# The inner layer of the second block's MLP in two groups of four products on four row tiles

## The chip, the cores and the metric

The kernel runs on one core of a Trainium2 chip. The metric is the device time of one launch in microseconds (us). TensorE (PE in the profile) multiplies into PSUM; VectorE (DVE) and ScalarE (ACT) read PSUM and work in SBUF; GpSimd (POOL) works in SBUF; SyncE (SP) issues DMAs. Each engine runs its own instructions in order, and engines wait for each other by semaphores.

## The reference

The input x has 32 sequences of 128 tokens of 144 numbers. Three transformer blocks follow each other, with a rotation between the first and the second. Each block is adaptive layer norm, attention with 16 heads of 9 numbers, and an MLP of width 576. The third block has a mixture of four experts as its MLP. What matters here is the second block (`L2`):

```python
ada = silu(c) @ W_ada + b_ada
shift_msa, scale_msa, gate_msa, shift_mlp, scale_mlp, gate_mlp = split(ada, 6)
h = modulate(layernorm(x), shift_msa, scale_msa)
x = x + gate_msa * attention(h, W_qkv, b_qkv, W_proj, b_proj)
h = modulate(layernorm(x), shift_mlp, scale_mlp)
mlp = gelu(h @ W_fc1 + b_fc1, approximate=True) @ W_fc2 + b_fc2
x = x + gate_mlp * mlp
```

## The kernel before

**Tiling.** All is float32. A sequence (128 tokens) is one step of attention; four sequences are a group (`G = 4`), so every block has eight groups (`NG = 8`). The MLP's inner layer and the projection to q and k are done for a whole group: a product gives 128 output channels for 4 x 128 tokens, one PSUM bank of 128 x 512. The width 576, a row for the bias of the outer layer and padding make five such chunks (`NFC = 5`); the fifth is half full.

**Main and rest.** The 144 input channels are more than TensorE's 128 rows. So each product is a main one over 128 channels (`hM`) and a rest over the other 16 and the bias (`hR`), accumulated in one bank. A rest needs 32 rows only. `hR` and the rest weights lie in four copies of 32 rows each, and a rest names one of the four row tiles (`rows4(k)`), so that rests on different tiles can run together. `both` (L716) issues a list of main products and a list of rests, rests first or main products first. Chunk m of the MLP uses tile `m % 3`; the three products of q and k use tiles 0, 1 and 2.

**PSUM.** One bank is for the weighted values (`ps_o`); seven banks are handed out in turn by `bank` (L82) to everything else. A tile waits for the last reader of the bank that it is given.

**The order.** It is written out by hand. The loop at L1439 runs over ticks; a tick has one sequence in each of three stages of attention. In order it issues the first half of `scores` (the maxima's products `ps_s` of one sequence and the exponentials' products `ps_w` of the one before; DVE takes the negated maxima `nm`, L930, and ACT the exponentials, L934), `weigh` (L940), the second half of `scores`, then `largest_T` (L867: PE transposes `nm`) and `largest` (L872: DVE adds it to q). Between these are named gaps, in order: a, e, t, first half of scores, stats, weigh, o, b0, b, den, pre1, second half of scores, c, y1, y2, y3, `largest_T`, z, d. In the second and third blocks the projection of attention follows d, but in every fourth tick of the second block it comes ahead of `largest_T`. `put` (L1308) hangs a function on a tick and a gap; `put2` (L1311) hangs its two halves. `sums_by_blocks` (L970) divides by the softmax's sums on DVE: it reads `on`, which ACT copies from `ps_o` (L955), and stands ahead of the second half's `nm` in DVE's queue.

**The lines that the change touches.** t0 is the tick at which a group's attention starts. In the second block (L1387 to L1391) `mlp1`, by `fc1` (L1020), does chunks 0 to 2 in gap c of tick t0 + 8 and chunks 3 and 4 in gap c of t0 + 9, rests first in both. `fc1` then activates a dummy number (L1034), which draws the load of the Gelu table on ACT, and the chunks (L1037) into `hid`; the next exponential draws the load of the Exp table. `mlp2` (L1049, L1039) is five products per sequence, in order of m, the last with `hid[:, SHARED]`, the fifth chunk. The four sequences' `mlp2` stand at t0 + 10 in gaps b and d, and t0 + 11 in b and c. The group three later has its q and k (`qk_chunks`, L753) in gap c of t0 + 10; ACT copies them (L766 to L776), and SP's four DMAs (L779) move a part of k. In the groups with a later group to rotate, `rotate_T` (L1054), `rotate_in` (L1071) and `rotate` (L1087) stand at t0 + 8 in d and t0 + 9 in b and d. `mlp` (L1594) lays the rest weights out on the host.

Of the kernel before, what the change touches and what calls it, by code (L numbers as in the profile page):

```python
# [17 lines left out]
B, T, C = 32, 128, 144  # L18
# [6 lines left out]

SHARED = 8
NPC = 9
MLP_COLS = NFC * (128 + 128 + C)
PAIR_COLS = NPC * (256 + C)
D = 64  # L30
E = 4
G = 4
# [37 lines left out]
def tile_kernel(ctx: ExitStack, tc: tile.TileContext, a: dict, out: bass.AP):  # L70
# [675 lines left out]
    def qk_tiles(g):  # L746
# [3 lines left out]
            gr[g]["kT"] = take_kT()  # L750
        return gr[g]["qT"], gr[g]["kT"]

    def qk_chunks(g):  # L753


        p = PARAMS[g[0]]
        hM, hR = gr[g]["hM_a"], gr[g]["hR_a"]
        qT, kT = qk_tiles(g)
        pss = [bank([128, G * T], f"ps_qk_{g[0]}_{g[1]}_{m}") for m in range(3)]
        cols = [slice(128 * m, 128 * m + 128) for m in range(3)]  # L760
        yield from both(
            [(ps, p.wqk[:, c], hM) for ps, c in zip(pss, cols)],
            [(ps, p.wqkR[rows4(m), cols[m]], hR[rows4(m)]) for m, ps in enumerate(pss)],
            False,
        )
        nc.scalar.copy(qT[:, 0, :], pss[0])  # L766
        if g[0] == 1 and g[1] < 2:
            nc.gpsimd.tensor_copy(kT[:, 3, :], kmask[:, 3:4].to_broadcast([128, G * T]))
        if g == (1, 0):
            for r in (1, 2):  # L770
                nc.scalar.mul(kT[:, r, :], pss[1], kmask[:, r : r + 1])
            gr[g]["k"] = kT, pss[1]
        else:
            nc.scalar.mul(kT[:, 2, :], pss[1], kmask[:, 2:3])
            nc.scalar.copy(kT[:, 1, :], pss[1])  # L775
        nc.scalar.copy(qT[:, 1, :], pss[2])  # L776
        for j in range(4):
            r = 32 * j + 1
            nc.sync.dma_start(  # L779
                kT[r : r + HD, 3, :], qT[r + PITCH : r + PITCH + HD, 1, :]  # L780
            )
# [235 lines left out]
        layer, b, g, i = of(s)  # L1017
        residual(b, st[s].pop("pj"), gr[g]["ga"][:, i, :], f"a_{s}", layer == 0)

    def fc1(g, p, name, m, to, rest_first):  # L1020


        hM, hR = gr[g]["hM_m"], gr[g]["hR_m"]
        pss = [bank([128, G, T], f"ps_h_{name}_{m + i}") for i in range(len(to))]
        cols = [slice(128 * (m + i), 128 * (m + i) + 128) for i in range(len(to))]
        tiles = [rows4((m + i) % 3) for i in range(len(to))]
        yield from both(
            [(ps, p.w1[:, c], hM) for ps, c in zip(pss, cols)],
            [(ps, p.w1R[r, c], hR[r]) for ps, c, r in zip(pss, cols, tiles)],
            rest_first,  # L1030
        )

        t = small.tile([128, 1], F32, tag="gelu", name=f"gelu_{name}_{m}", bufs=1)
        nc.scalar.activation(t, half, AF.Gelu_apprx_tanh)  # L1034
        for ps, i in zip(pss, to):
            n = 64 if g[0] < 2 and i == SHARED else 128
            nc.scalar.activation(hid[:n, i], ps[:n], AF.Gelu_apprx_tanh)  # L1037
# [6 lines left out]
        return ps  # L1044

    def mlp1(g, m, to, rest_first):
        return fc1(g, MLPS[g[0]], f"{g[0]}_{g[1]}", m, to, rest_first)

    def mlp2(g, i):  # L1049
        b = g[1] * G + i  # L1050
# [113 lines left out]
                nc.gpsimd.tensor_tensor(acc, acc, t, ALU.add)  # L1164

    def moe1(g, pair, part, rest_first):
        to = ((0, 1, 2), (SHARED, 3, 4), (5, 6, 7))[part]
        return fc1(g, PAIRS[pair], f"3_{g[1]}_{pair}", 3 * part, to, rest_first)

    def shared_by_gate(g, pair):  # L1170

# [154 lines left out]
    for layer in range(3):  # L1326
        ahead = 5 if layer == 0 else 6
        for n in range(NG):
            g = (layer, n)
            t0 = first[layer] + n * G  # L1330
            for i in range(G):
                s = layer * B + n * G + i
                at_a = t0 + i - ahead
                if layer == 1 and n == 0:
                    at_a = t0 - 4 + i // 2
                if layer == 1 and i == 0:
                    put(at_a - 2, "d", rotate_T, n)
                    put(at_a - 1, "b", rotate_in, n)
                    put(at_a - 1, "d", rotate, n)
                stats[at_a].append((s, "a"))  # L1340
                stats[t0 + i + 3].insert(0, (s, "m"))
                if layer < 2:
                    end = at_a != t0 + i - ahead or (layer, i) == (1, G - 1)
                    put(*((at_a, "d") if end else (at_a + 1, "b")), ln_T, s, "a")
                else:
                    put(at_a, "d", ln_T, s, "a")
                if layer == 0:
                    put(t0 + i + 4, "a", ln_T, s, "m")
                else:
                    put(t0 + i + 3, "d", ln_T, s, "m")  # L1350
                if layer == 0:
                    put(t0 + i - 3, "c", qk0_project, s)
                    put(t0 + i - 3, "z", qk0_variance, s)
                    put(t0 + i - 2, "e", qk0_guess, s)
                    if s == 0:
                        for gap in "bbc":
                            put(-2, gap, qk0_newton, s, nc.vector)
                    else:
                        for gap in ("b", "c", "y2"):
                            put(t0 + i - 2, gap, qk0_newton, s)  # L1360
                    put(t0 + i - 1, "b", qk0_divide, s)
                    put(t0 + i - 1, "c", qk0_T, s)
            if layer == 0:
                for i in (0, 2):
                    put2(t0 + i // 2, "stats", "b", values, g, i, 2, True)
            elif layer == 1:
                put2(t0, "stats", "b", values, g, 0, 2, True)
                put2(t0 + 1, "stats", "b", values, g, 2, 2, True)
            else:
                put2(t0, "y2", "y2", values, g, 0, 2, True)  # L1370
                put2(t0 + 1, "den", "pre1", values, g, 2, 2)
            if layer:
                put2(t0 - 2, "c", "c", qk_chunks, g)
                if g == (1, 0):
                    put(t0 - 2, "y2", qk_masked, g)
                if g != (1, 0):
                    for r in (0, 1):
                        put(*((t0 - 2, "z") if layer == 2 and n > 2 else (t0 - 1, "a")), qk_mask, g, nc.gpsimd, r)
            if layer == 0:
                joined = t0 + 10 >= first[1]  # L1380
                put2(t0 + 10, *("cc" if joined else ("stats", "b")), mlp1, g, 0, (0, 1, 2), True)
                joined = t0 + 11 >= first[1]
                put2(t0 + 11, *("cc" if joined else "dd"), mlp1, g, 3, (3, SHARED), joined)
                for i in range(G):
                    at_ = t0 + 12 + i // 2 + ((n, i) == (NG - 1, G - 1))
                    put(at_, "bd"[i % 2] if at_ < first[1] or (n, i) == (NG - 2, G - 1) else "bc"[i % 2], mlp2, g, i)
            elif layer == 1:  # L1387
                put2(t0 + 8, "c", "c", mlp1, g, 0, (0, 1, 2), True)
                put2(t0 + 9, "c", "c", mlp1, g, 3, (3, SHARED), True)
                for i in range(G):  # L1390
                    put(t0 + (10, 10, 11, 11)[i], "bdbc"[i], mlp2, g, i)  # L1391
            else:
                put2(t0 + 7, "o", "c", gate_logits, g)
                put(t0 + 8, "e", expert_ranks, g)
                put(t0 + 8, "stats", expert_weights, g)
                for i in range(G):
                    put(t0 + 8 + i // 2, "cdab"[i], moe_bias, g, i, n == NG - 1)
                for pair in range(2):
                    at_ = t0 + 8 + 2 * pair
                    put2(at_, "stats", "b0", moe1, g, pair, 0, True)  # L1400
                    if n == NG - 1:
                        put2(at_, "stats", "pre1", moe1, g, pair, 1, True)
                    else:
                        put2(at_, "den", "pre1", moe1, g, pair, 1, False)
                    put2(at_ + 1, "stats", "b0", moe1, g, pair, 2, True)
                    put2(at_, "stats", "y1", shared_by_gate, g, pair)
                    put2(at_, "y2", "y3", moe2_parts, g, 2 * pair, 0)
                    put(at_ + 1, "b", moe2, g, 2 * pair, 1)
                    put(at_ + 1, "c", moe2, g, 2 * pair, 2)
                    put(at_ + 1, "y2", moe2, g, 2 * pair, 3)  # L1410
                    for i in range(G):
                        put(at_ + 2, "aabb"[i], moe2, g, 2 * pair + 1, i)
                        if pair and n == NG - 1:
                            put(at_ + 2, "aabb"[i], moe_out, g, i, nc.vector if i == G - 1 else nc.gpsimd)
                if n < NG - 1:
                    put(t0 + 12, "b", moe_out, g)
# [256 lines left out]
```

## Time and profile before

| what | us |
|---|---|
| median of 3 runs (lowest, highest) | 1279.36 (1277.12, 1282.75) |
| the profiled execution | 1276.88 |
| its span, first to last instruction | 1275.2 |
| a period of four ticks, second block, groups with rotation | 37.4 |
| ScalarE's table loads, all: 57 at L934 and 58 at L1034 | 73.1 and 74.4 |
| ScalarE's idle time before L1037, put down to the products of fc1 | 99.4 |
| VectorE's busy time at L930, the maxima | 246.5 |
| mean granted TensorE clock | 0.989 of full |

Busy time is summed over instructions and their overlap is taken out per engine. A line of the timeline gives start, length, engine, line, operation, output<-input, partitions x elements, count, and in brackets the idle time before it with what ended it. A float32 matmul shows as two instructions, so x6 is three products. Matmuls overlap their neighbours in the pipeline: the distance from one start to the next says more than the length.

### The profile page before, as it was taken

To read this page: it belongs to the slowest core of one execution; us is meant where nothing else is said; L and a number is where in the kernel's file an instruction comes from. 1 tells how busy PE (TensorE), PEld (TensorE's weight loads), DVE (VectorE), ACT (ScalarE), POOL (GpSimd) and SP (SyncE) were. 2 spreads that over 40 slices of the span, in tenths; PEclk is the share of its full clock that TensorE was granted. 3 is DMA by queue.
4 is the path that set the end of the run, shared out by engine and by line. 5 is a ranking of instruction groups with operands and counts; after the bars stand their busy time and mean duration, and the time that the engine had idled before them with its cause. 6 is when DMAs were issued, how large, how long until landed. Compare 5 with 4: busy or idle time off the path is not lost.

```text
span 1275.2 us, 35382 instructions
## 1 busy us (share of the span) xinstructions
PE 1226.3 (96%) x13980; PEld 898.6 (70%) x13980; DVE 808.1 (63%) x2540; ACT 779.4 (61%) x1724; POOL 667.9 (52%) x1641
## 2 busy tenths in 40 slices
PE   6889888999989999999999999999999999999998
PEld 4668666778766677767677777767676767677666
DVE  5598888877875466666666766645454646454343
ACT  2467777688776665667666666565656555555431
POOL 5567777766754444444545554626262636261610
PEclk9699999999999999999999999999999999999999
DMA  8301011010013111111121111210101010100000
GB/s 227 75 4 38 3 37 37 2 38 21 20 36 132 56 39 55 35 49 45 41 87 56 56 47 46 85 47 15 51 11 55 11 55 11 55 20 17 20 27 10
DMA packets 50328, 56.49 MB, mean 44 GB/s; under 512 B 4560, under 2 KB 35792, under 8 KB 49904
## 3 DMA queue, kind: packets, MB, share of 16 engines
q1 hardware_dynamic: 49504, 53.75, 14.2%
q8 instruction: 113, 1.85, 0.6%
q10 hardware_dynamic: 656, 0.44, 0.2%
q14 instruction: 55, 0.45, 0.1%
HBM read 39.99 MB, written 13.00 MB: 42 GB/s over the span
## 4 chain that ended last, share of the span: by engine, by line
PE 70%; DVE 4%; ACT 0%; issue 0%; POOL 0%; DVEq 0%
PE ps_h L721 20%; PE ps_f L1191 10%; PE ps_s L918 7%; PE ps_w L918 6%; PE ps_o L949 6%; PE ps_qk L721 5%; PE ps_f L1043 4%; PE ps_pj L1013 3%; PE ps_v L721 3%; PE ps_f L1196 1%; DVE nm L930 1%; PE ps_o L870 1%; PE ps_hT_m L690 1%; PE ps_cw L1179 1%; PE ps_hT_a L690 1%; PE ps_d L1092 0%
## 5 line engine op out<-in xcount | busy, mean ns | idle before, releaser
L930 DVE TENSOR_REDUCE nm<-ps_s 128x4 f32<-128x512 f32 x384 | 246.5, 683 | 95.9 <-PE ps_w L918 74.8
L934 ACT ACTIVATE pr<-ps_w 128x512 f32<-128x512 f32 x384 | 208.5, 595 | 149.7 <-PE ps_w L918 141.0
L918 PE MATMUL ps_s<-kT,qT 32*128 32x256 f32 (+2 forms) x1536 | 235.1, 409 | 0.9 <-ACT kT L850 0.9
L918 PE MATMUL ps_w<-q,kT 32*128 32x128 f32 x3072 | 230.0, 284 | 0.0
L918 PEld LDWEIGHTS ps_w<-q,kT 32*128 32x128 f32 x3072 | 194.4, 187 | 11.0 <-issue 6.2
L1037 ACT ACTIVATE hid<-ps_h 128x512 f32<-128x512 f32 (+1 forms) x224 | 120.4, 590 | 99.8 <-PE ps_h L721 99.4
L918 PEld LDWEIGHTS ps_s<-kT,qT 32*128 32x128 f32 x1536 | 136.9, 187 | 29.4 <-issue 9.2
L721 PE MATMUL ps_h<-hM_m,mlps 128*128 128x512 f32 x304 | 144.1, 607 | 0.0
L1200 DVE SCALAR_TENSOR_TENSOR acc<-ps_f,cw,acc 128x144 f32<-128x144 f32 x128 | 46.7, 365 | 146.3 <-PE ps_f L1191 71.5
L999 POOL TENSOR_TENSOR x_sb<-x_sb,res_a 128x144 f32<-128x144 f32 x96 | 46.9, 489 | 156.5 <-DVE res_a L1002 155.8
L949 PE MATMUL ps_o<-pr,vaug 128*32 128x128 f32 x3072 | 104.4, 277 | 0.0
L949 PEld LDWEIGHTS ps_o<-pr,vaug 128*32 128x32 f32 x3072 | 78.6, 110 | 32.7 <-PE ps_w L918 17.4
L721 PEld LDWEIGHTS ps_h<-hM_m,mlps 128*128 128x128 f32 x304 | 53.4, 190 | 66.9 <-issue 65.6
L1043 PE MATMUL ps_f<-mlps,hid 128*128 128x144 f32 x640 | 93.7, 294 | 0.0
L1043 PEld LDWEIGHTS ps_f<-mlps,hid 128*128 128x128 f32 x640 | 82.4, 191 | 8.8 <-issue 4.7
L934 ACT ACT_TABLE_LOAD x57 | 73.1, 1283 | 10.0 <-PE ps_w L918 9.1
L793 POOL TENSOR_SCALAR kT<-kT,cst 128x512 f32<-128x512 f32 x30 | 46.9, 1562 | 58.5 <-ACT kT L775 57.0
L1034 ACT ACT_TABLE_LOAD x58 | 74.4, 1283 | 1.0
L661 POOL TENSOR_SCALAR rs_m_a<-mv_m_a 128x2 f32<-128x2 f32 x81 | 15.5, 191 | 113.5 <-DVE mv_m_a L659 86.6
L1191 PEld LDWEIGHTS ps_f<-pair,hid 128*128 128x128 f32 x512 | 66.9, 190 | 8.4 <-issue 7.6
L701 ACT ACTIVATE hM_m<-ps_hT_m,modM 128x128 f32<-128x128 f32 x96 | 44.6, 465 | 45.8 <-PE ps_hT_m L690 43.8
L1191 PEld LDWEIGHTS ps_f<-mlps,hid 128*128 128x128 f32 x512 | 66.7, 190 | 7.9 <-issue 6.9
(336 smaller groups left out, 2756.2 us busy)
## 6 DMA issues: line engine op xcount, KB each, us to landing
gates<-gates SPq DMA_DIRECT2D x48, 288.0 KB
hD_m<-hG_m SPq DMA_DIRECT2D x24, 256.0 KB
hR_m<-hD_m SPq DMA_DIRECT2D x24, 256.0 KB
hD_a<-hG_a SPq DMA_DIRECT2D x16, 256.0 KB
hR_a<-hD_a SPq DMA_DIRECT2D x16, 256.0 KB
x_sb<-in_x SPq DMA_DIRECT2D x8, 288.0 KB
out_x<-x_sb SPq DMA_DIRECT2D x7, 288.0 KB
mlps<-in_L_mlp SPq DMA_DIRECT2D x2, 1000.0 KB
```

Source lines behind the costliest of these rows:

```text
L721: nc.tensor.matmul(ps, x, y, start=k == 0, stop=k == 1)
L793: eng.tensor_scalar(o, k, m, None, ALU.mult)
L918: nc.tensor.matmul(o, x, y, start=True, stop=True)
L930: nc.vector.tensor_reduce(to, view, AX.X, ALU.max, negate=True)
L934: nc.scalar.activation(pr[:, 4 * e : 4 * e + 4, :].rearrange("p s q -> p (s q)"), view, AF.Exp, scale=SCALE,)
L949: nc.tensor.matmul(po[rows4(j), t, :], v[:, 4 * j + 2 * t + r, :], prs[j // 2][:, 4 * (j % 2) + 2 * r + t, :], start=r == 0, stop=r == 1,)
L999: nc.gpsimd.tensor_tensor(x_sb[:, b, :], x_sb[:, b, :], t, ALU.add)
L1034: nc.scalar.activation(t, half, AF.Gelu_apprx_tanh)
L1037: nc.scalar.activation(hid[:n, i], ps[:n], AF.Gelu_apprx_tanh)
L1043: nc.tensor.matmul(ps, hid[:, at0, i, :], w2[:, m, :], start=m == 0, stop=m == NFC - 1)
L1191: nc.tensor.matmul(ps[:, 0, :], hid[:, at0 + m, i, :], w2[:, at0 + m, :], start=m == 0, stop=m == 3)
L1200: nc.vector.scalar_tensor_tensor(acc, ps[:, 0, :], w, acc, ALU.mult, ALU.add)
```

## The change

Chunks 0 to 3 of the second block's inner layer are issued together in gap c of t0 + 8, main products first, with their rests on row tiles 0 to 3. The fifth chunk is issued with q and k: `qk_chunks` of the group three later (for the last three groups, one of the first three groups of the third block) takes one more main product and one more rest, on tile 3, and after its own copies activates that chunk. Gap c of t0 + 9 is left without products. The four `mlp2` move to t0 + 10 in gap d, and t0 + 11 in b, c and d. A table `MLP_TILES` gives the row tiles; the first block's and those of the third block's first pair of experts are as before, and those of the second pair are others. The parts of `moe1` beyond 2 are not called, and the branch for the third block's MLP in `qk_chunks` isn't reached.

```diff
+MLP_TILES = {
+    "L0": (0, 1, 2, 0, 1), "L2": (0, 1, 2, 3, 3),
+    "L3_0": (0, 1, 2, 0, 1, 2, 0, 1, 2), "L3_1": (1, 2, 3, 3, 0, 1, 0, 2, 3),
+}
...
+    JOIN = {(1, n): (1, n - 3) for n in range(3, NG)}
+    JOIN.update({(2, n): (1, n + NG - 3) for n in range(3)})
...
     def qk_chunks(g):
...
-        yield from both(
-            [(ps, p.wqk[:, c], hM) for ps, c in zip(pss, cols)],
-            [(ps, p.wqkR[rows4(m), cols[m]], hR[rows4(m)]) for m, ps in enumerate(pss)],
-            False,
-        )
+        main = [(ps, p.wqk[:, c], hM) for ps, c in zip(pss, cols)]
+        rest = [(ps, p.wqkR[rows4(m), cols[m]], hR[rows4(m)]) for m, ps in enumerate(pss)]
+        f = JOIN.get(g)
+        if f is not None:
+            l, mlp, m = ("L2", MLPS[1], 4) if f[0] == 1 else ("L3_1", PAIRS[1], 3)
+            psh, main_h, rest_h = fc1_products(f, l, mlp, f"{f[0]}_{f[1]}_s", (m,))
+            main, rest = main + main_h, rest + rest_h
+        yield from both(main, rest, False)
...
         nc.scalar.copy(qT[:, 1, :], pss[2])
+        if f is not None:
+            gelus(f, f"{f[0]}_{f[1]}_s", psh, m, (SHARED,))
...
-    def fc1(g, p, name, m, to, rest_first):
+    def fc1_products(g, l, p, name, ms):
         hM, hR = gr[g]["hM_m"], gr[g]["hR_m"]
-        tiles = [rows4((m + i) % 3) for i in range(len(to))]
+        pss = [bank([128, G, T], f"ps_h_{name}_{m}") for m in ms]
+        cols = [slice(128 * m, 128 * m + 128) for m in ms]
+        tiles = [rows4(MLP_TILES[l][m]) for m in ms]
+        main = [(ps, p.w1[:, c], hM) for ps, c in zip(pss, cols)]
+        rest = [(ps, p.w1R[r, c], hR[r]) for ps, c, r in zip(pss, cols, tiles)]
+        return pss, main, rest
+
+    def fc1(g, l, p, name, ms, to, rest_first):
+        pss, main, rest = fc1_products(g, l, p, name, ms)
+        yield from both(main, rest, rest_first)
+        gelus(g, name, pss, ms[0], to)
+
+    def gelus(g, name, pss, m, to):
         t = small.tile([128, 1], F32, tag="gelu", name=f"gelu_{name}_{m}", bufs=1)
         nc.scalar.activation(t, half, AF.Gelu_apprx_tanh)
         for ps, i in zip(pss, to):
...
             elif layer == 1:
-                put2(t0 + 8, "c", "c", mlp1, g, 0, (0, 1, 2), True)
-                put2(t0 + 9, "c", "c", mlp1, g, 3, (3, SHARED), True)
+                put2(t0 + 8, "c", "c", mlp1, g, 0, (0, 1, 2, 3), False)
                 for i in range(G):
-                    put(t0 + (10, 10, 11, 11)[i], "bdbc"[i], mlp2, g, i)
+                    put(t0 + (10, 11, 11, 11)[i], "dbcd"[i], mlp2, g, i)
...
-    def mlp(name, w1, b1, w2):
+    def mlp(name, w1, b1, w2, tiles):
...
-            k, cols = m % 3, slice(128 * m, 128 * m + 128)
+            k, cols = tiles[m], slice(128 * m, 128 * m + 128)
```

More of the change, by code (lines that the diff above doesn't have):

```diff
@@ L1018, in project_sum @@
         residual(b, st[s].pop("pj"), gr[g]["ga"][:, i, :], f"a_{s}", layer == 0)
-    def fc1(g, p, name, m, to, rest_first):
+    def fc1_products(g, l, p, name, ms):
         hM, hR = gr[g]["hM_m"], gr[g]["hR_m"]
-        pss = [bank([128, G, T], f"ps_h_{name}_{m + i}") for i in range(len(to))]
-        cols = [slice(128 * (m + i), 128 * (m + i) + 128) for i in range(len(to))]
-        tiles = [rows4((m + i) % 3) for i in range(len(to))]
[L1027 to L1031, printed above, removed]
+        pss = [bank([128, G, T], f"ps_h_{name}_{m}") for m in ms]
[9 more added lines that the diff above has]
+    def gelus(g, name, pss, m, to):
         t = small.tile([128, 1], F32, tag="gelu", name=f"gelu_{name}_{m}", bufs=1)
@@ L1046, in mlp1 @@
     def mlp1(g, m, to, rest_first):
-        return fc1(g, MLPS[g[0]], f"{g[0]}_{g[1]}", m, to, rest_first)
+        ms = range(m, m + len(to))
+        return fc1(g, ("L0", "L2")[g[0]], MLPS[g[0]], f"{g[0]}_{g[1]}", ms, to, rest_first)
     def mlp2(g, i):
@@ L1166, in moe1 @@
     def moe1(g, pair, part, rest_first):
-        to = ((0, 1, 2), (SHARED, 3, 4), (5, 6, 7))[part]
-        return fc1(g, PAIRS[pair], f"3_{g[1]}_{pair}", 3 * part, to, rest_first)
+        ms = range(3 * part, 3 * part + 3)
+        if part > 2:
+            ms = ((0, 1, 2, 4), (5, 6, 7, 8))[part - 3]
+        to = [(0, 1, 2, SHARED, 3, 4, 5, 6, 7)[m] for m in ms]
+        return fc1(g, f"L3_{pair}", PAIRS[pair], f"3_{g[1]}_{pair}", ms, to, rest_first)
     def shared_by_gate(g, pair):
@@ L1609 @@
         w2 = np.vstack([w2, b2, pad[:63, :1].repeat(C, 1)])
-        mlp(l, np.hstack([w1, pad[:C]]), np.hstack([b1, pad[C]]), w2)
+        mlp(l, np.hstack([w1, pad[:C]]), np.hstack([b1, pad[C]]), w2, MLP_TILES[l])
     for n in range(2):
@@ L1619 @@
         w2 = np.vstack([w2[0][:512], w2[1][:512], w2[0][512:], w2[1][512:]])
-        mlp(f"L3_{n}", w1, b1, w2)
+        mlp(f"L3_{n}", w1, b1, w2, MLP_TILES[f"L3_{n}"])
     arrays["L3_b2"] = inputs["L3_cond_b2"].ravel()
```

## The prediction

> **What bounds the kernel now.** I read the page first: busy shares and the chain that ended last.
>
> ```profile
> PE 1226.3 (96%) x13980; PEld 898.6 (70%) x13980; DVE 808.1 (63%) x2540; ACT 779.4 (61%) x1724; POOL 667.9 (52%) x1641
> ...
> PE 70%; DVE 4%; ACT 0%; issue 0%; POOL 0%; DVEq 0%
> ```
>
> TensorE (PE) sets the time: anything PE waits for is paid in full, and removed PE work is gained only if nothing else ends later. So I walked one 4-tick period of the second block in the timeline, engine by engine. It repeats every 37.4 us (tables of windows: 37.26 of 37.40 us PE busy in three of them). I name ticks by their distance from t0 of the MLP's own group: T8 to T11. PE first (start us, length us, engine, line, op, out<-in, shape, count):
>
> ```profile
> 511.51 1.07 PE L721 MATMUL ps_h<-hR_m,mlps 32*128 32x512 f32 x6
> 512.50 2.84 PE L721 MATMUL ps_h<-hM_m,mlps 128*128 128x512 f32 x6
> 515.18 0.27 PE L870 MATMUL ps_o<-cst,nm 128*128 128x128 f32 x1
> ...
> 521.72 1.02 PE L721 MATMUL ps_h<-hR_m,mlps 32*128 32x512 f32 x4
> 522.67 1.98 PE L721 MATMUL ps_h<-hM_m,mlps 128*128 128x512 f32 x4
> 524.50 0.27 PE L870 MATMUL ps_o<-cst,nm 128*128 128x128 f32 x1
> ...
> 528.76 1.49 PE L1043 MATMUL ps_f<-mlps,hid 128*128 128x144 f32 x10
> ...
> 534.06 1.14 PE L721 MATMUL ps_qk<-hR_a,L_wqkR 32*128 32x512 f32 x6
> 535.13 0.33 PE L870 MATMUL ps_o<-cst,nm 128*128 128x128 f32 x1
> 535.29 1.39 PE L1043 MATMUL ps_f<-mlps,hid 128*128 128x144 f32 x10
> 536.52 0.27 PE L690 MATMUL ps_hT_m<-cst,xh_m 128*128 128x128 f32 x1
> ```
>
> From start to next start: rests of three chunks 0.99, of two 0.95, of q and k 1.07; a main product about 0.9; one mlp2 1.23 to 1.42. L870 is the transpose of the row maxima nm, after which PE does the rest of its tick. In T9 the two fc1 chunks (521.72 to 524.50) stand just before it, and cover this on VectorE (DVE):
>
> ```profile
> 520.50 0.45 DVE L974 STREAM_TRANSPOSE block<-on 128x256 f32<-128x256 f32 x1
> ...
> 522.17 1.28 DVE L930 TENSOR_REDUCE nm<-ps_s 128x4 f32<-128x512 f32 x2
> ```
>
> nm is ready at 523.45, 1.7 us after the scores end. Last ScalarE (ACT):
>
> ```profile
> 512.89 1.28 ACT L1034 ACT_TABLE_LOAD   x1
> 514.18 0.20 ACT L1034 ACTIVATE gelu<-half 128x1 f32<-128x1 f32 x1
> 514.29 1.69 ACT L1037 ACTIVATE hid<-ps_h 128x512 f32<-128x512 f32 x3
> ...
> 517.83 1.28 ACT L934 ACT_TABLE_LOAD   x1 [0.86 <-PE ps_w L918]
> ...
> 535.22 0.58 ACT L766 COPY qT<-ps_qk 128x512 f32<-128x512 f32 x1 [2.64 <-PE ps_qk L721]
> ```
>
> The load back to Exp waits for PE's scores; it isn't hidden. The four copies of q and k take 2.0 us (535.22 to the next op at 537.22).
>
> **The change, step by step** (group at 511.51; each figure is how much later, +, PE then stands than before).
>
> PE work alone: three groups of rests, 0.99 + 0.95 + 1.07 = 3.01, become two of four. No row shows four tiles of 512 columns; between 0.95 (two tiles) and 1.07 + 0.9 = 1.97 (the fourth alone), nearest the rows of three: I take 1.1 each. Saved: 0.8 us a group, 6.5 us in eight. All main products, mlp2s, gelus (five a group) and table loads (two each way) remain, so the rest is order.
>
> *T8 and T9.* With the rests last, all four chunks end together, at 511.51 + 3.6 + 1.1 = 516.2; before, the first gelu ran at 514.29, during the main products. Now four gelus, 0.53 apart, end at 518.4; then come hM_m and, in the groups with a rotation, xM and xR, queued behind them on ACT, which took 1.10 us, to 519.5. Only then the Exp load (1.28), the two Exps (1.09) and the copy of on, which starts 0.1 before they end and takes 0.38: 522.1. DVE's block to nm takes 2.95 (520.50 to 523.45): nm is there at 525.1, against PE's transpose at 524.50 before. That is +0.65, though PE has 1.9 us less to do by then: T9's fc1 chunks, its cover, are gone. Four h tiles hold four of seven PSUM banks; if the next scores wait for the last gelu and for hM_m, PE is 1.3 later at the scores, the chain about 0.7 later: +1.35. I take +1.0. In the four groups without rotation (h at 661.27, transpose at 673.25 before) the same sum gives +1.05.
>
> [...]
>
> *T10.* The first mlp2 leaves gap b: -1.42. A wait of 0.35 in its scores (526.40 to the weighing at 527.75, against 1.0 normally) goes, since no gelu stands before them on ACT: -0.35 in rotated groups. The q and k group has a fourth main product, +0.92, and +0.03 of rests. PE is at the transpose at +0.2.
>
> *The stall I count most on.* In gap d, right behind the transpose, stands the first mlp2. Its fifth product reads hid[SHARED], which now comes from this same group of products. ACT needs for it 0.09 + 2.0 (four copies) + 1.28 (Gelu load) + 0.11 + 0.59 = 4.07 us from the end of the products; PE has 0.16 (transpose) + 0.98 (four products). It waits 2.9 us, with the transposes of hT_m, the projection and the next scores queued behind it: +3.1 at T11.
>
> *T11.* ACT's load back to Exp again waits for ps_w, so the Exps are 1.28 later than PE is, then on, block, nm: nm ready at about 547.4, PE there at 547.45. A tie; before, PE waited 0.1 there. Then the mlp2 moved from T10's b to here, +1.42, less 0.45, since it covers the wait of the next scores for q (544.62 to 546.17, 1.55 instead of 1.1).
>
> Sum of a group: 1.0 - 1.42 - 0.35 + 0.95 + 2.95 + 0 + 1.42 - 0.45 = +4.1; without rotation 0.4 more, +4.5. 4 x 4.1 + 4 x 4.5 = +34 us. The saving of 0.8 is in it already.
>
> At no cost: the DMAs of kT stay behind qT's last copy on SP, POOL's masks of kT behind ACT's copies, which keep their place; hG_m with its two DMAs comes about 4 us later, and hR_m is wanted two ticks (18 us) on; without that cover PE would wait the same 4. mlp2's residuals come a gap later, and the third block's statistics read x_sb more than ten ticks on. The third block's other row tiles (24 groups of rests) may overlap the scores' tail more or less, 0.1 us each by the overlaps around 508.30: between -2.4 and +2.4, taken as 0.
>
> *Clock.* Idle PE is slowed here. At 78.95 to 80.73 it waited for DVE, and (window, its us, PE, PEld, DVE, ACT, POOL busy, then PEclk):
>
> ```profile
> 79.00:80.00 1.00, 0.00 (x0) 0.00 (x0) 0.86 (x6) 0.69 (x2) 0.90 (x3) 1.00 0.00 0
> ...
> 83.00:84.00 1.00, 1.00 (x17) 0.78 (x11) 0.93 (x4) 0.00 (x0) 0.94 (x3) 0.50 0.00 0
> 84.00:85.00 1.00, 1.00 (x11) 0.90 (x8) 0.96 (x5) 0.84 (x2) 0.81 (x3) 0.94 0.00 0
> ```
>
> 1.77 us of idling were followed by 3.1 us at half clock (80.85 to 83.95), at most 1.55 us lost; a wait of 1.38 at 58.5 had none. Waits of 2.9 and 1.8 us a group can each set it off: 0 to 3.1 us. ACT's lag in T11 hides part; I take 0.5, +4 in all.
>
> [...]
>
> **The sum.** The profiled execution took 1276.88 (span 1275.2 and 1.7 around it), 2.5 under the median of 1279.36. 1276.9 + 34 + 4 = 1315.
>
> **Rivals.** *The saving arrives* (faster): PE loses 0.8 a group, the waits are covered: 1276.9 - 6.5 = 1270. For it: 96% PE, a chain of PE alone. Against: the fifth product's wait is a data dependence on an in-order queue. It needs ACT's 4.07 us to shrink to 1.9: no row does.
> *Half clock after both waits*, in all groups: 1277 + 34 + 25 = 1336. For it: the 1.77 us row; against: ACT's lag covers part.
> *Tiles don't run together*, what the change says not done: 2 x 0.9 more a group, +14: 1329. Against: two tiles 0.95, three 0.99.
> *Small loss*: the T8/T9 wait vanishes and only 2.5 of the last remain: 4.1 - 1.0 - 0.45 = 2.65 a group, 1298.
> *Break-even*: the waits just eat the 0.8: 1277.
>
> **How the numbers follow.** Forecast 1302 to 1326: 0.65. Half clock or serial tiles: 0.14. Small loss (from 1284): 0.11. Break-even 0.03. Faster 0.07. A measurement tells about 0.5%, 6.4 us, from no change: slower 0.90, same 0.03, faster 0.07. The range reaches from under the small loss to within the rivals above: 1295 to 1333.
>
> **What would show it.** PE's L870 in T9 waiting 1 to 2.5 us for nm; the last product of the first mlp2 waiting about 3 us for hid after a Gelu load that stands behind the copies of q and k; period 41 to 42 us instead of 37.4; PE busy share down to about 93%. Wrong if hid[SHARED] is there within 2 us of the q and k products, if nm is ready in T9 when the scores end, or if the rests of four take over 1.5 us.

## The result, and the profile after

| | us |
|---|---|
| median after, 6 runs (lowest, highest) | 1336.41 (1333.23, 1345.06) |
| median before, beside it, 6 runs (lowest, highest) | 1281.03 (1277.12, 1284.04) |
| ratio, 95% interval | 1.0448 (1.0412 to 1.0485) |
| the profiled execution after, its span | 1345.06, 1343.4 |

The changed kernel is slower by 55 us. That is the direction of the forecast, but above its range, which ended at 1333. The profiled execution happens to be the longest of the six, 8.7 us over their median, and the profiled one before is 4.2 under its own; so the two spans differ by 68.2 us where the medians differ by 55.4.

The page after, with the same busy line and chain as before:

```profile
PE 1256.4 (94%) x13980; PEld 923.2 (69%) x13980; DVE 809.2 (60%) x2540; ACT 783.1 (58%) x1724; POOL 670.9 (50%) x1641
...
PE 64%; DVE 5%; ACT 4%; issue 1%; DMA 0%; POOL 0%; ACTq 0%; DVEq 0%
```

PE has as many instructions, 13980, but 30 us more busy time: the same work took longer in places. And 4% of the chain is ACT now, where it was 0%. PE's waits say where (engine, tile and line <- what was waited for: us in total, times, longest us); first before, then after:

```profile
PE ps_o L870 <- DVE nm L930: 2.3, 5, 0.7
```

```profile
PE ps_f L1058 <- ACT hid L1052: 23.7, 8, 3.0
...
PE ps_o L882 <- DVE nm L942: 19.0, 15, 2.6
```

The first new wait is the fifth product of the first `mlp2`, once a group; the second is the transpose of the maxima, mostly in T9 (lines moved by 4 to 15 in the changed file: L870 is now L882, L1043 is L1058). One group of the changed kernel in PE's timeline, to be set against the lines of the group at 511.51 before:

```profile
518.88 3.70 PE L725 MATMUL ps_h<-hM_m,mlps 128*128 128x512 f32 x8
522.52 1.14 PE L725 MATMUL ps_h<-hR_m,mlps 32*128 32x512 f32 x8
523.59 0.33 PE L882 MATMUL ps_o<-cst,nm 128*128 128x128 f32 x1
...
525.01 1.20 PE L930 MATMUL ps_s<-kT,qT 32*128 32x384 f32 x4
...
532.95 0.30 PE L882 MATMUL ps_o<-cst,nm 128*128 128x128 f32 x1 [1.48 <-DVE nm L942]
...
542.84 0.33 PE L882 MATMUL ps_o<-cst,nm 128*128 128x128 f32 x1
543.00 1.15 PE L1058 MATMUL ps_f<-mlps,hid 128*128 128x144 f32 x8
547.11 0.51 PE L1058 MATMUL ps_f<-mlps,hid 128*128 128x144 f32 x2 [2.96 <-ACT hid L1052]
...
550.12 1.92 PE L961 MATMUL ps_o<-pr,vaug 128*32 128x128 f32 x32
```

Four rests take 522.52 to 523.59, so they do run together. Then nothing covers the transpose in T9, and the first `mlp2` splits into two lines, its fifth product 2.96 us late. The last line is a sign of the clock: the same 32 weighings take 1.08 elsewhere. ACT at the same place shows why the fifth product is late:

```profile
542.92 0.59 ACT L776 COPY qT<-ps_qk 128x512 f32<-128x512 f32 x1 [3.50 <-PE ps_h_s L725]
...
544.45 0.61 ACT L786 COPY qT<-ps_qk 128x512 f32<-128x512 f32 x1
545.08 1.28 ACT L1049 ACT_TABLE_LOAD   x1
546.37 0.20 ACT L1049 ACTIVATE gelu_s<-half 128x1 f32<-128x1 f32 x1
546.48 0.57 ACT L1052 ACTIVATE hid<-ps_h_s 64x512 f32<-64x512 f32 x1
```

ACT idles 3.50 us until the products are done, and only then makes its copies, loads the table and activates. PE's clock around this wait (window, its us, busy PE, PEld, DVE, ACT, POOL, then the granted clock):

```profile
546.00:547.00 1.00, 0.00 (x0) 0.00 (x0) 0.00 (x0) 0.99 (x3) 0.00 (x0) 1.00 0.07 18
...
548.00:549.00 1.00, 1.00 (x15) 0.85 (x17) 0.31 (x1) 0.69 (x2) 0.73 (x2) 0.74 0.13 33
549.00:550.00 1.00, 1.00 (x20) 0.90 (x14) 0.00 (x0) 0.00 (x0) 1.00 (x2) 0.50 0.46 129
550.00:551.00 1.00, 1.00 (x24) 0.82 (x24) 0.81 (x2) 0.68 (x1) 0.90 (x2) 0.50 0.48 139
551.00:552.00 1.00, 1.00 (x21) 0.60 (x13) 0.96 (x4) 0.99 (x2) 1.00 (x1) 0.55 0.07 15
552.00:553.00 1.00, 1.00 (x12) 1.00 (x9) 0.29 (x2) 0.96 (x3) 0.83 (x3) 1.00 0.00 0
```

PE is at half clock for some 3.4 us *after* the wait, while it is fully busy. I add 1 minus the granted clock over windows of 1 us from 400 to 920 us and call the sum clock-time lost: 0 before, 23.9 us after, which is 14 such stretches of 1.7 us. (Ahead of 400 us, where both kernels do the same work, it is 13.7 before and 3.4 after, so the mean granted clocks, 0.989 and 0.980, show less of this.)

From one Gelu load of T8 to the next, the eight periods were 37.4 (four times), 35.3, 34.5, 35.6 and 35.0 us; they are 43.7, 42.3, 43.6, 43.6, 44.7, 44.6, 45.1 and 43.2. The differences (6.2, 4.9, 6.1, 6.2, 9.4, 10.2, 9.6 and 8.3 by the unrounded starts) sum to 60.8 of the span's 68.2 us. Nearly all of the rest, 7.2, lies ahead of the first T8, where both kernels do the same work; there the executions of other kernels differ by several us too (e2's first T8, below, comes 5.1 earlier than that of the kernel before). The second group had no clock loss: its 4.9 are waits alone. Eight such groups would make 39 us, but the last four, without rotation, wait longer; e2 puts the sum at 41. That leaves some 20 us to the clock in this execution, and 55.4 - 41 = 14 in the medians.

### The profile page after: what moved, and what is told of

It reads as the page before. It is cut to its first block, busy times and chain, and to the rows that moved or that the text cites. A ratio compares the mean times of both kernels' runs of the same rounds, so it can differ in the third digit from the quotient of the medians.

```text
span 1343.4 us, 35379 instructions
## 1 busy us (share of the span) xinstructions
PE 1256.4 (94%) x13980; PEld 923.2 (69%) x13980; DVE 809.2 (60%) x2540; ACT 783.1 (58%) x1724; POOL 670.9 (50%) x1641
## 4 chain that ended last, share of the span: by engine, by line
PE 64%; DVE 5%; ACT 4%; issue 1%; DMA 0%; POOL 0%; ACTq 0%; DVEq 0%
PE ps_h L725 17%; PE ps_f L1210 9%; PE ps_s L930 7%; PE ps_w L930 6%; PE ps_o L961 5%; PE ps_qk L725 4%; PE ps_f L1058 3%; PE ps_pj L1025 3%; PE ps_v L725 2%; DVE nm L942 2%; PE ps_f L1215 1%; PE ps_o L882 1%; ACT pr L946 1%; ACT L1049 1%; PE ps_hT_m L694 1%
## 5 line engine op out<-in xcount | busy, mean ns | idle before, releaser
L930 PE MATMUL ps_s<-kT,qT 32*128 32x256 f32 (+2 forms) x1536 | 247.7, 423 | 0.9 <-ACT kT L862 0.9
L930 PE MATMUL ps_w<-q,kT 32*128 32x128 f32 x3072 | 240.6, 292 | 0.0
L930 PEld LDWEIGHTS ps_w<-q,kT 32*128 32x128 f32 x3072 | 203.5, 195 | 9.0 <-issue 3.6
L1052 ACT ACTIVATE hid<-ps_h 128x512 f32<-128x512 f32 (+1 forms) x216 | 115.2, 593 | 115.7 <-PE ps_h L725 115.7
L930 PEld LDWEIGHTS ps_s<-kT,qT 32*128 32x128 f32 x1536 | 144.5, 194 | 34.6 <-issue 16.2
L725 PE MATMUL ps_h<-hM_m,mlps 128*128 128x512 f32 x288 | 135.1, 605 | 0.0
L1058 PE MATMUL ps_f<-mlps,hid 128*128 128x144 f32 x640 | 95.7, 295 | 23.7 <-ACT hid L1052 23.7
L961 PE MATMUL ps_o<-pr,vaug 128*32 128x128 f32 x3072 | 109.7, 286 | 0.0
L1058 PEld LDWEIGHTS ps_f<-mlps,hid 128*128 128x128 f32 x640 | 83.5, 192 | 33.0 <-ACT hid L1052 25.4
L961 PEld LDWEIGHTS ps_o<-pr,vaug 128*32 128x32 f32 x3072 | 82.3, 114 | 34.4 <-PE ps_w L930 17.7
L705 ACT ACTIVATE hM_m<-ps_hT_m,modM 128x128 f32<-128x128 f32 x96 | 44.7, 466 | 73.7 <-PE ps_hT_m L694 63.7
L1011 POOL TENSOR_TENSOR x_sb<-x_sb,res_m 128x144 f32<-128x144 f32 x64 | 32.7, 511 | 95.3 <-DVE res_m L1014 94.8
```

The costliest lines, as they stand in the source:

```text
L725: nc.tensor.matmul(ps, x, y, start=k == 0, stop=k == 1)
L930: nc.tensor.matmul(o, x, y, start=True, stop=True)
L961: nc.tensor.matmul(po[rows4(j), t, :], v[:, 4 * j + 2 * t + r, :], prs[j // 2][:, 4 * (j % 2) + 2 * r + t, :], start=r == 0, stop=r == 1,)
L1011: nc.gpsimd.tensor_tensor(x_sb[:, b, :], x_sb[:, b, :], t, ALU.add)
L1058: nc.tensor.matmul(ps, hid[:, at0, i, :], w2[:, m, :], start=m == 0, stop=m == NFC - 1)
```

## The experiments

My theory: the two waits, and the half clock behind them, are the whole loss. Rivals: the other row tiles of the third block cost something; the half clock lies under waits and costs nothing; the waits merely move when one is removed. Each edit is to the changed kernel. The runs stood beside the kernel before at 1281.14 us (first four), 1277.73 (the next four) and 1278.80 (last two); comparisons between them go by ratios.

**e1: the fifth chunk's gelu ahead of the copies of q and k.** The table load then falls into ACT's idle 3.50 us.

```diff
+        if f is not None:
+            gelus(f, f"{f[0]}_{f[1]}_s", psh, m, (SHARED,))
         nc.scalar.copy(qT[:, 0, :], pss[0])
...
-        if f is not None:
-            gelus(f, f"{f[0]}_{f[1]}_s", psh, m, (SHARED,))
```

> The activation of the fifth chunk stands ahead of ScalarE's four copies of q and k, so its table load runs while TensorE still multiplies. Theory (the loss is waits on an in-order queue, and the half clock that follows them): the wait of 2.96 us before the fifth product of the first mlp2 falls under 0.3 us in all eight groups, -21 to -24 us, and the half clock behind it goes too, -10 to -15 us: 1298 to 1306 us against 1336. Rival (rests on four tiles, or the third block's other tiles, are what costs): the wait goes, but the time stays above 1325.

Measured: 1301.60 us, ratio 1.0165 (1.0113 to 1.0218). PE's timeline of e1 shows the `mlp2` behind the transpose in one piece, where the kernel after had it split:

```profile
578.54 0.33 PE L882 MATMUL ps_o<-cst,nm 128*128 128x128 f32 x1
578.70 1.39 PE L1058 MATMUL ps_f<-mlps,hid 128*128 128x144 f32 x10
579.93 0.27 PE L694 MATMUL ps_hT_m<-cst,xh_m 128*128 128x128 f32 x1
```

and ACT's timeline has the load done before the products are:

```profile
575.14 1.28 ACT L1049 ACT_TABLE_LOAD   x1
576.44 0.20 ACT L1049 ACTIVATE gelu_s<-half 128x1 f32<-128x1 f32 x1
578.67 0.59 ACT L1052 ACTIVATE hid<-ps_h_s 64x512 f32<-64x512 f32 x1 [2.03 <-PE ps_h_s L725]
```

The fifth product's wait is gone, the other is unchanged (19.0 us), and the clock-time lost falls from 23.9 to 10.2. So an order of four lines on ACT cost about 36 us (1.0448 - 1.0165 = 0.0283 of 1281): 24 of waiting, the rest clock.

**e2: useless products in the two waits.** They change no wait's end, and keep PE busy.

```diff
+    def fill_pe(g, n):
+        ps = bank([128, G * T], f"ps_fill_{g[0]}_{g[1]}_{n}")
+        for i in range(n):
+            nc.tensor.matmul(ps, ident, gr[g]["hM_m"], start=True, stop=True)
...
+                put(t0 + 9, "c", fill_pe, g, 2)
+                put(t0 + 10, "d", fill_pe, g, 3)
```

> TensorE gets work that no one reads: two 512-column products in gap c of T9 and three right before the first mlp2 in T10, both where it waits in the changed kernel. It does more, and no wait of another engine is shortened. Theory (half clock after the waits costs some 20 us): granted clock back to 0.989, waits replaced by the useless products, 1313 to 1322 us against 1336. Rival (the half clock is hidden behind ScalarE's lag, as the prediction assumed): 1331 us or more, faster by 0 to 5.

Measured: 1321.61 us, ratio 1.0346 (1.0301 to 1.0391). PE's timeline of e2 at the second place, and its waits:

```profile
530.85 2.74 PE L1073 MATMUL ps_fill<-hM_m,cst 128*128 128x512 f32 x6
533.43 1.14 PE L1058 MATMUL ps_f<-mlps,hid 128*128 128x144 f32 x8
534.96 0.51 PE L1058 MATMUL ps_f<-mlps,hid 128*128 128x144 f32 x2 [0.39 <-ACT hid L1052]
```

```profile
PE ps_o L882 <- DVE nm L942: 5.9, 13, 0.9
...
PE ps_f L1058 <- ACT hid L1052: 3.1, 8, 0.4
```

The products fill 2.6 us of the wait; ACT's work that it waits for is untouched. The clock-time lost is 0.0, and the kernel is faster by 14.8 us in the medians, 13 by the ratios. Nothing else that was added could make it faster, so this is what the half clock cost.

e2's trace also separates waits from clock, group by group. From one Gelu load of T8 to the next:

| group | 0 | 1 | 2 | 3 | 4 | 5 | 6 | 7 | sum |
|---|---|---|---|---|---|---|---|---|---|
| e2, longer than before (no clock lost) | 4.9 | 4.9 | 4.9 | 4.9 | 5.2 | 5.7 | 5.2 | 5.2 | 41.0 |
| after, longer than e2 | 1.3 | -0.1 | 1.2 | 1.2 | 4.2 | 4.5 | 4.4 | 3.1 | 19.8 |
| clock-time lost, after | 1.7 | 0 | 1.7 | 1.7 | 5.1 | 5.1 | 5.1 | 3.4 | 23.9 |

The second line follows the third: of the clock-time lost, five sixths were paid, and one sixth lay under something else.

**e3: other row tiles for the third block's second pair.** `"L3_1": (0, 1, 2, 0, 1, 2, 0, 1, 2)`, as before the change.

> Only the second expert pair's row tiles are put back to m % 3. Theory (they cost nothing): within 4 us of the changed kernel, 1332 to 1340 us. Rival (the other order of tiles delays the third block's rests): 10 us or more below it.

Measured: 1339.31 us, ratio 1.0487 (1.0438 to 1.0536), the same as after. This part of the change costs nothing that can be measured, as was forecast. Its second block is that of the kernel after, so its trace shows how much the clock varies between executions: clock-time lost 17.1 us, with periods that are 13.6 longer than e2's. Three of its groups lost none, and there the periods are within 0.2 of e2's, as they must be if the useless products cost next to nothing.

**e4: an `mlp2` back as cover in T9.** The last `mlp2` of a group moves to the next group's T9, gap c, where the fc1 chunks were. `hid` takes turns between two halves for this.

```diff
-                put2(t0 + 8, "c", "c", mlp1, g, 0, (0, 1, 2, 3), False)
+                put2(t0 + 8, "c", "c", mlp1, g, 0, [4 * (n % 2) + i for i in range(4)], False)
...
-                    put(t0 + (10, 11, 11, 11)[i], "dbcd"[i], mlp2, g, i)
+                    if n < NG - 1:
+                        put(t0 + (10, 11, 11, 13)[i], "dbcc"[i], mlp2, g, i)
+                    else:
+                        put(t0 + (10, 11, 11, 11)[i], "dbcd"[i], mlp2, g, i)
...
-        ps = fc2(g, MLPS[g[0]].w2, i, 0, f"{g[0]}_{b}")
+        ps = fc2(g, MLPS[g[0]].w2, i, 4 * (g[0] * g[1] % 2), f"{g[0]}_{b}")
```

> Second block: odd groups use the free half of hid, and the fourth sequence's mlp2 moves from T11's gap d to gap c of the next group's T9 (not in the last group). Theory (T9's wait for nm comes from the empty gap c): the wait of 1.5 to 2.6 us there falls by up to 1.4 us in seven groups, -8 to -10 us, and with it the half clock after it, -5 to -10: 1317 to 1324 us. Rival (the wait is set by ScalarE's lag from T8 and moves along): within 4 us of 1336.

Measured: 1330.21 us, ratio 1.0384 (1.0330 to 1.0438). PE's waits in e4:

```profile
PE ps_f L1058 <- ACT hid L1052: 23.7, 8, 3.0
...
PE ps_o L882 <- DVE nm L942: 9.1, 12, 1.6
```

The wait for nm falls by 9.9 us and the clock-time lost to 17.1, but the gain is 6 to 8 us where 12 to 19 were expected: a miss in size. The moved `mlp2` had covered, at its old place, the next scores' wait for q. With it gone these scores start only 0.36 us after the transpose (597.82 to 598.18) and take 1.1 instead of 1.0. That is the likely taker of a part. In the two profiled executions the eight periods differ by more, 11.9 us, so another part may be how much clock the other executions lost; I haven't separated them.

**e5: e1 and e4 together.**

> Both edits that helped: the fifth chunk's activation ahead of the copies of q and k, and the fourth mlp2 in gap c of the next group's T9. Theory (two separate waits, each with its half clock): the gains add, no wait for hid, the waits for nm about 9 us instead of 19, clock-time lost under 5 us: 1287 to 1294 us. Rival (one lag behind both): within 4 us of 1301.6.

Measured: 1289.30 us, ratio 1.0083 (1.0054 to 1.0111). By the ratios e1 gains 0.028, e4 0.006, both 0.037: the two waits are separate losses, and the removal of one doesn't bring the other out. In the trace, 8.9 us of waits for nm remain and a clock-time lost of 1.7.

**e6: rests in the middle.** On e5, the four rests (and those of q, k and the fifth chunk) stand between two halves of the main products, so that the first banks are complete early and gelus and copies start during the products.

```diff
+        if rest_first is None:
+            h = len(main) // 2
+            for ps, x, y in main[:h]:
+                nc.tensor.matmul(ps, x, y, start=True, stop=False)
+            yield
+            for i, (ps, x, y) in enumerate(rest):
+                nc.tensor.matmul(ps, x, y, start=i >= h, stop=i < h)
+            for ps, x, y in main[h:]:
+                nc.tensor.matmul(ps, x, y, start=False, stop=True)
+            return
...
-            main, rest = main + main_h, rest + rest_h
-        yield from both(main, rest, False)
+            main, rest = main_h + main, rest_h + rest
+        yield from both(main, rest, False if f is None else None)
```

> As the run before, and in both groups of four the main products of two chunks come first, then the four rests together, then the other two main products; so two chunks (in the second group the fifth chunk and the first third of q and k) are complete some 1.8 us before the group ends. Theory (what is left in T8 and T9 is ScalarE's late start, since with the rests last all four chunks end together): the rest of the waits for nm falls below 3 us and T9's scores start 0.5 to 0.9 us earlier, -8 to -13 us: 1276 to 1284 us. Rival (PSUM banks or VectorE set T9): within 4 us of the run before.

Measured: 1292.14 us, ratio 1.0094 (1.0063 to 1.0126): no gain over e5. The rests of q and k now come earlier, and in the trace they wait for `hR_a`, which a DMA brings: the products 1.5 us, their weight loads (which overlap other products) 4.9; the waits for nm are 10.6.

**e7 and e8: the Exp table loaded early.** A dummy exponential at the end of the ticks after T8 and T10 (and every second tick of the block) draws the load before the scores are done. e7 is that on e1, e8 on e6.

```diff
+        if first[1] + 8 <= tick < first[1] + B + 8 and (tick - first[1]) % 2 == 0:
+            t = small.tile([128, 1], F32, tag="exp", name=f"exp_{tick}", bufs=1)
+            nc.scalar.activation(t, half, AF.Exp)
```

> The changed kernel with the fifth chunk's activation first, and the dummy Exp, but neither the cover in T9 nor the mixed order. Theory (T9's wait for nm begins with ScalarE's lag from T8, of which the Exp load's wait for the scores is 0.3 to 0.5 us): the waits for nm fall from 19 to 14 to 16 us, -3 to -6 us against 1301.6: 1295 to 1299 us. Rival (the empty gap alone sets it): within 2 us of 1301.6.

> As the run before, and a dummy Exp at the end of T8 and T10 draws the load of the Exp table while ScalarE would wait for the scores. Theory: the exponentials of the next tick start 0.5 to 1.3 us earlier after each Gelu; what of that TensorE still waits for is small by now, -1 to -5 us: 1272 to 1281 us. Rival (nothing waits for ScalarE there any more): within 2 us of the run before.

Measured: e7 1298.81 us, ratio 1.0144 (1.0101 to 1.0187); e8 1288.63, ratio 1.0072 (1.0044 to 1.0100). e7's time is in its theory's range, but not for its reason: the wait for nm is 19.1, where it was 19.0 without the dummy, and its ratio isn't clear of e1's. In its first T9 the maxima begin at 525.82, just as the scores end (525.79), and PE still waits 1.43 us: with nothing between the scores and the transpose the maxima themselves set the wait there, which is the rival's reason. e8 misses: 8.4 us of waits for nm and 1.4 for `hR_a` remain (6.0 at the weight loads for `hR_a`), as PE's waits from 480 to 880 us show:

```profile
PE ps_o L891 <- DVE nm L951: 8.4, 10, 1.4
PE ps_qk L727 <- DMA hR_a<-hD_a: 1.4, 3, 0.8
```

**e9: rests of q and k last again, the `mlp2` spread.** On e8; they stand at t0 + 11 in b and c, t0 + 13 in c and t0 + 14 in b.

```diff
-            main, rest = main_h + main, rest_h + rest
-        yield from both(main, rest, False if f is None else None)
+            main, rest = main + main_h, rest + rest_h
+        yield from both(main, rest, False)
...
-                        put(t0 + (10, 11, 11, 13)[i], "dbcc"[i], mlp2, g, i)
+                        put(t0 + (11, 11, 13, 14)[i], "bccb"[i], mlp2, g, i)
```

> As the run with the early Exp, but q, k and the fifth chunk have their rests last again, and the four mlp2 stand in T11's b and c and, but for the last group, in the next group's T9 in c and T10 in b. Theory (what was left was T9's wait for nm where no rotation fills the tick, and q's rests that come before the DMA of hR_a has landed, since T10 had lost its mlp2 in b): the wait for hR_a goes from 6 us to under 1, -4 to -9 us: 1279 to 1285 us. Rival (the order inside the groups of four, or the tiling mode's changes, cost as much as the shared rests save): within 3 us of 1288.6.

Measured: 1290.76 us, ratio 1.0109 (1.0067 to 1.0151). The wait for `hR_a` is gone, and the waits for nm are 11.6: no gain, as the rival said. Of its two causes, no run shows what a change of the tiling mode costs.

**e10: e9 in the first four groups, the others in the order before the change** (chunks 0, 1 and 3 in T8, 2 and 4 in T9, because of their row tiles; q and k alone).

> The same for the first four groups of the second block only, the ones whose ticks T8 and T9 have a rotation; the other four have the order of the kernel before (three chunks in T8, two in T9, q and k alone). Theory (the groups with a rotation gain 0.4 us of their period, as two of them showed, the others lose 1 to 3): within 4 us of the kernel before, 1274 to 1281 us against 1278, so no gain that can be measured. Rival (the order pays where the tick is full): 1270 us or less.

Measured: 1280.50 us, ratio 1.0030 (1.0005 to 1.0054): no better than before. The traces say where e9's loss lay: its eight periods are 13.5 us longer than before, 1.8 in the four groups with rotation and 11.7 in the four without; with the old order in those, e10 keeps 1.9 and 2.1. No version here beats the kernel before. In e5, e6, e8 and e9 some 9 to 14 us are left, of which the waits for nm (8 to 12, against 2.3) make most; where the saved 6.5 us of rests go in these versions stays open.

## Why the prediction was wrong in its size

*The step that failed* is the clock: "ACT's lag in T11 hides part; I take 0.5, +4 in all". e2 measures this term by itself: 13 to 15 us, and the traces have 13.6 (e3) and 19.8 (after), so 1.6 to 2.5 a group and not 0.5. The mechanism was right, half clock behind the two waits. The hiding was not: ACT's lag hides a fifth to a sixth of the clock-time lost, not five sixths. Tick by tick against e2, 8.5 of 10.2 us were paid behind T9's waits and 11.9 of 13.7 behind the fifth product's. The upper bound of 3.1 us a group was low as well: the stretch behind the row at 79 us is 3.4 us long (80.7 to 84.1, not 80.85 to 83.95), and beside some waits the slow stretch is twice as long (719.1 to 726.0 us in the trace after), so three groups lost 5.1.

The sum missed the median by 21 us: 10 of them are this term, 7 the waits, and 4 the start, since it began at the profiled execution's 1276.9 and the median before is 1281.0.

What came is the rival *half clock after both waits*, which stood at 1336 and was given, with serial tiles, 0.14. It has the place and the cause. That its time agrees to 1 us is luck: its terms stood at 34 and 25 and came as 41 and 14, on a start that was 4 lower.

*The waits* were 41 for the forecast 34: 4.9 a group with rotation for 4.1, and 5.2 to 5.7 without for 4.5. By steps, in groups 0 and 1:

- Rests of four: 1.07 and 1.08 us, 0.86 saved a group (forecast 1.1 each, 0.8 saved). Right; so the saving came in PE's work.
- T9's transpose: +1.08 in group 0, with a wait of 1.48 (forecast +1.0). Right, and by the chain that was named: the scores spread to 1.9 us (525.01 to 526.91), probably as they wait for banks that the gelus free (one weight load there waits 0.2 us for hid; no other wait is listed), and the Exp load stands at 527.25. Without rotation the waits are 2.1 to 2.6.
- T10's transpose: +0.34 and +0.48 (forecast +0.2).
- The fifth product: 2.96 in every group (forecast 2.95). The `mlp2` is longer by 3.2 (group 1: 586.82 to 591.27, against 1.23 before): the last product, standing alone, pays 0.26 more that overlapped before.
- T11: the transpose starts at +3.75, with a wait for nm of 0.2 to 0.3 in it (forecast a tie).
- The moved `mlp2`: +1.1 net, so its cover of the next scores' wait was worth 0.24 to 0.3 and not 0.45. Group 1 ends at +4.86 for the forecast 4.1.

Three small terms (T10, the fifth product, the moved `mlp2`), each on the low side, make most of the 0.76 a group.

*The other rivals.* Serial tiles are excluded by the 1.07. The small loss needed T9's wait to vanish; in no version does it do so in every group, and e4 cuts the sum to half. That the saving arrives is excluded by the trace, and even with one wait gone and the other halved (e5) the kernel isn't faster.

*The period* was forecast at 41 to 42 us for 37.4. It is 42.3 in the one group without clock loss and 43.6 with one slow stretch, which was the first sign of where the forecast was short. PE's share, 94% and not 93%, hid this: slowed products count as busy (1.00 busy at a clock of 0.50 from 549 to 551 us).

## What to carry to other kernels

Before work is moved away from the front of an instruction, ask what that work covers: here two fc1 chunks covered VectorE's maxima, and the fifth chunk's distance covered a table load. Once the loss is known, look at the order on the engine that is late; putting a table load and one activation ahead of four copies, into time in which ACT idled anyway, won back 36 of 55 us. And a wait of 2 to 3 us on TensorE can cost more than its length: in two traces of the same second block the half clock behind such waits lost 17 and 24 us, and some four fifths of it were paid. Don't take most of it as hidden unless a trace shows the cover.

## What the runs showed of the hardware

In the trace after, from 500 to 880 us, the granted clock is 0.50 in eleven stretches: eight of 3.4 us and three of 6.8. Each begins near the end of one of TensorE's waits, between 1.0 us ahead of it (794.24 us, the wait ended at 795.27) and 1.6 us behind it (842.03 us and 840.41). Not every wait has such a stretch:

| trace | TensorE waits for | us | waits with a stretch at 0.50 | without |
|---|---|---|---|---|
| before | VectorE, L379 | 1.77 | 1 (80.7 to 84.1 us) | 0 |
| after | `hid`, fifth product | 2.96 | 7 | 1 (ended at 590.92 us) |
| after | `nm` in T9, with rotation | 1.48 to 1.55 | 0 | 4 |
| after | `nm` in T9, without rotation | 2.11 to 2.62 | 4 | 0 |
| e1 | `nm` in T9, the second and third group | 1.48 | 1 (609.4 to 612.8 us) | 1 (ended at 568.65 us) |

So the length of a wait alone doesn't tell: 2.96 us stand on both sides, and so do 1.48. The executions differ as well: with the same second block, and 23.7 us of waits for `hid` in both, the clock-time lost is 23.9 us in the trace after and 17.1 in e3's, where three groups have no stretch at all.

Useless products made this kernel faster: with five more of 128 x 512 a group, e2 took 13 to 15 us less than the kernel after, and its clock-time lost is 0.0.
